# Fixed PSUM banks for the two halves of a convolution block in a four-layer kernel

## Chip, cores and metric

One Trainium2 chip, one core. The time is the device time of one launch in microseconds (us), the median of three runs. The profile is one further execution with the hardware profiler on.

## What is computed

`x` is a float32 tensor (4, 48, 256, 256). Four layers follow each other, each of the form "normalise in 16 groups of 3 channels, apply the layer, add the input". Cut to what matters:

```python
# layer 0: channel attention (48x48) over a 1x1 and a 3x3 depthwise convolution, then a 1x1 projection
x = x + L0(gn(x))
# layer 1: the tensor re-read as tokens of 48 consecutive numbers
t = gelu(gelu(tokens @ W1 + b1))          # 48 -> 16
x1, x2 = t[..., :8], t[..., 8:]
n = layernorm(x2)                         # over 8
g = x1 * (depthwise3x3(n) * pointwise(n))
x = x + (g @ W2 + b2)                     # 8 -> 48, as (h, w, channel)
# layers 2 and 3: four sweeps over rows and columns, each step
# new = input + conv1d(old, w, 5 taps) + b
x = x + L2(gn(x));  x = x + L3(gn(x))
```

Once the attention matrix of layer 0 is known, its output is a 3x3 convolution of the normalised input with weights that the kernel computes per image. That convolution is what "the convolution" means below.

## The kernel before

The work stands in four stretches of the span.

1. 0 to about 1635 us: `products` sums, for each of the four images, the products that the attention needs (L294 to L296).
2. About 1635 to 3205 us: the convolution of layer 0, 64 blocks of 16 rows (16 blocks an image). From about 1980 us the token layer (`gated_layer`, layer 1) runs among it, for images whose convolution is done.
3. 3205 to 3570 us: the rest of the token layer, with the first steps of the sweeps.
4. 3570 us to the end: the sweeps of layers 2 and 3 (`scans`, L1048 and what follows it).

**A convolution block** (`block`, L565) holds eight pairs of rows in four PSUM tiles, numbered c = 0 to 3, each one bank (2 x 256 float32 in each of 96 partitions). `full(c)` (L572) takes a bank and puts three matmuls into it (L582, from `x1n`); `rest(q)` (L586) adds six more matmuls, three each for the tiles q and q + 2 (L591, from `x2n`, 64 partitions each, two at a time on the array). So tiles 0 and 2 are the block's first half, tiles 1 and 3 its second. After `rest`, VectorE adds the input (L605) and takes statistics (L606) of each tile, which frees its bank. The input of the next block is normalised on ScalarE (L542) into `x1n` and `x2n`, of which there is one buffer each.

**The token layer** goes through 32 items in 34 ticks (`tick`). In a full tick one item gets its hidden layer (tiles `ph`, L701), the next one is transposed (`relay` copies the loaded tokens on GpSimd into `pairs`, L748; six tiles `ptok`, L754, of four transposes each, copied to SBUF by VectorE L760 or ScalarE L758), and an older one is gated and written (`psp` and `pch`, L833 to L836; `pm` L788; `pvar` L797, read by ScalarE's L799; eight tiles `pout`, L871, to which VectorE adds the input `xr`, L882, two instructions a tile, after ScalarE's L857 has added the bias to `xr`). A tick calls `conv` four times, and each call is half a block: two blocks a tick.

[...] One (`p_small`) is for small products. Seven are handed out in the convolution and the token layer by a ring of pools:

```python
own = ctx.enter_context(tc.tile_pool(name="a_banks", bufs=5, space=PSUM))
banks = Ring([spare] * 2 + [own] * 5)
```

`Ring.tile` (L125) asks for the pools in turn: two tiles from `spare`, then five from `own`, and so on, whatever the tiles are for. `spare` (2 banks) is later needed by the sweeps of the first pair of images, so when the last convolution half has been handed out (`if not todo`, L646) the ring is cut to `own`.

**The order of instructions** on each engine isn't written by hand. The kernel's text gives a priority order, a planner goes through it with estimated durations, and when an instruction's bank isn't free yet in its plan it takes later instructions first. So the way banks are handed out decides two things: which earlier tile a new one has to wait for, and the order in which TensorE's instructions stand in the program. Each engine then takes its instructions in that order.

## Time and profile before

| | us |
|---|---|
| median of 3 runs | 9344.98 (9341.82 to 9350.19) |
| the profiled execution | 9345.89 |
| its span, first to last instruction | 9344.1 |
| TensorE busy, whole span | 8855.4 (95%) |
| VectorE busy | 4375.0 (47%) |
| ScalarE busy | 3344.1 (36%) |
| GpSimd busy | 1455.0 (16%) |
| mean granted TensorE clock | 0.971 |

The profile's page gives busy time by engine, the span in 40 slices, the chain of work that ended last and the costliest groups of instructions. Beside it the trace answers questions on a stretch: a timeline (start, length, engine, line, operation, and in brackets the idle time before it and what ended it), the waits of one engine added up, and the busy time and granted clock of any window. TensorE's name in these is PE, VectorE's DVE, ScalarE's ACT, GpSimd's POOL; SPq is the queue that issues the DMAs.

### The profile page before, as it was taken

How to read it: one execution, taken by the hardware profiler on the slowest of the kernel's cores; microseconds unless marked ns; L12 is line 12 of the kernel's file. 1: busy time of each engine (PE TensorE's matmuls, PEld its weight loads, DVE VectorE, ACT ScalarE, POOL GpSimd, SP SyncE). 2: the span in 40 equal slices, each digit the busy share in tenths (PEclk: the TensorE clock that was granted, in tenths of full speed). 3: DMA queues.
4: the chain of work that ended last, by engine and by line, in shares of the span. 5: the costliest groups of instructions: out<-in, count | busy, mean ns of one | idle time of the engine just before them, and what ended most of it. 6: DMA issues, size and time to landing. Idle time of an engine off the chain costs nothing.

```text
span 9344.1 us, 160472 instructions
## 1 busy us (share of the span) xinstructions
PE 8855.4 (95%) x62920; PEld 7293.6 (78%) x62920; DVE 4375.0 (47%) x10798; ACT 3344.1 (36%) x7053; POOL 1455.0 (16%) x2866
## 2 busy tenths in 40 slices
PE   6999999999999889999999999999999999999982
PEld 4777777333333348999999999999999999988981
DVE  3331010334555464445666544555677555445541
ACT  0011000123333356645433465555333433445200
POOL 0000000001111120000143200000233333100462
PEclk9999999999999899999999999999999999999996
DMA  7663322568877868666477676654776787697799
GB/s 150 131 131 83 75 65 60 118 138 173 173 167 168 180 151 174 135 143 170 122 173 187 136 159 133 158 140 130 190 190 171 165 193 180 135 213 191 204 217 194
DMA packets 1058039, 1440.82 MB, mean 154 GB/s; under 512 B 64976, under 2 KB 981200, under 8 KB 991232
## 3 DMA queue, kind: packets, MB, share of 16 engines
q1 hardware_dynamic: 1057184, 1430.23, 67.3%
q8 instruction: 493, 8.08, 0.4%
q14 instruction: 266, 2.18, 0.1%
q0 software_dynamic: 96, 0.33, 0.0%
HBM read 837.19 MB, written 534.77 MB: 147 GB/s over the span
## 4 chain that ended last, share of the span: by engine, by line
PE 90%; DMA 4%; DVE 2%; SPq 1%; ACT 1%; issue 1%; POOL 1%; ACTq 0%; DVEq 0%; POOLq 0%
PE ps L1048 57%; PE py L582 7%; PE acc L294 5%; PE acc L295 5%; PE py L591 4%; PE acc L296 4%; PE pt L276 1%; PE ph L701 1%; PE pout L871 1%; PE ptok L754 1%; PE psp L833 1%; DMA oi<-x 1%; DMA tok<-x 1%; DMA sx<-in_x 1%; DMA stage<-x 1%
## 5 line engine op out<-in xcount | busy, mean ns | idle before, releaser
L1048 PE MATMUL ps<-carry,w 96*96 96x128 f32 x48960 | 5588.8, 275 | 91.0 <-DVE carry L1056 60.5
L1048 PEld LDWEIGHTS ps<-carry,w 96*96 96x96 f32 x48960 | 5451.9, 163 | 233.5 <-DVE carry L1056 92.9
L1056 DVE SCALAR_TENSOR_TENSOR carry<-ps,b,col 96x128 f32<-96x128 f32 x4080 | 1777.1, 439 | 1139.7 <-PE ps L1048 964.9
L1261 POOL TENSOR_TENSOR stage<-stage,carry 96x128 f32<-96x128 f32 (+1 forms) x2044 | 1055.3, 520 | 3803.3 <-DVE carry L1056 3621.0
L1231 ACT COPY col<-carry 96x128 f32<-96x128 f32 x2040 | 859.7, 425 | 986.9 <-DVE carry L1056 985.7
L1128 ACT ACTIVATE dn<-carry,b 96x128 f32<-96x128 f32 (+1 forms) x2044 | 791.2, 399 | 1059.2 <-DVE carry L1052 1056.7
L1052 DVE TENSOR_TENSOR carry<-ps,dn 96x128 f32<-96x128 f32 x2280 | 651.6, 287 | 744.9 <-PE ps L1048 571.1
L1052 DVE TENSOR_TENSOR carry<-ps,up 96x128 f32<-96x128 f32 x1792 | 516.3, 288 | 654.0 <-ACT up L1169 491.4
L582 PE MATMUL py<-x1n,wy 128*96 128x512 f32 x1536 | 729.1, 626 | 25.0 <-ACT x1n L542 22.7
L1169 ACT COPY up<-carry 96x128 f32<-96x128 f32 x1792 | 531.0, 298 | 582.3 <-DVE carry L1052 566.5
L294 PE MATMUL acc<-xt 128*96 128x288 f32 x2048 | 666.9, 409 | 0.0
L295 PE MATMUL acc<-xs,xt 128*96 128x288 f32 x2048 | 666.9, 407 | 0.0
L582 PEld LDWEIGHTS py<-x1n,wy 128*96 128x96 f32 x1536 | 255.5, 172 | 457.0 <-issue 443.4
L279 DVE COPY xt<-pt 128x384 f32<-128x384 f32 x256 | 136.5, 554 | 852.2 <-PE pt L276 651.8
L296 PE MATMUL acc<-xt,xs 128*96 128x192 f32 x2048 | 501.7, 327 | 0.0
L261 ACT ACTIVATE xn<-raw,coef 96x2048 f32<-96x2048 f32 x64 | 133.6, 2094 | 985.6 <-PE pt L276 819.1
L296 PEld LDWEIGHTS acc<-xt,xs 128*96 128x96 f32 x2048 | 332.2, 165 | 154.4 <-issue 1.5
L605 DVE TENSOR_TENSOR y<-py,t 96x512 f32<-96x512 f32 x256 | 170.4, 679 | 601.4 <-PE py L591 601.4
L295 PEld LDWEIGHTS acc<-xs,xt 128*96 128x96 f32 x2048 | 332.1, 164 | 151.2 <-issue 2.4
L591 PE MATMUL py<-x2n,wy 64*96 64x512 f32 x1536 | 367.8, 601 | 0.0
L294 PEld LDWEIGHTS acc<-xt 128*96 128x96 f32 x2048 | 330.6, 165 | 5.4 <-issue 1.1
L591 PEld LDWEIGHTS py<-x2n,wy 64*96 64x96 f32 x1536 | 118.3, 158 | 226.4 <-issue 226.2
(177 smaller groups left out, 4194.2 us busy)
## 6 DMA issues: line engine op xcount, KB each, us to landing
stage<-x SPq DMA_DIRECT2D x64, 1536.0 KB
x<-stage SPq DMA_DIRECT2D x64, 1536.0 KB
dn<-x SPq DMA_DIRECT2D x240, 384.0 KB
R<-col SPq DMA_DIRECT2D x60, 1536.0 KB
col<-U SPq DMA_DIRECT2D x60, 1536.0 KB
col<-R SPq DMA_DIRECT2D x60, 1536.0 KB
D<-dn SPq DMA_DIRECT2D x56, 1536.0 KB
up<-D SPq DMA_DIRECT2D x56, 1536.0 KB
```

Source lines behind the costliest of these rows:

```text
L294: nc.tensor.matmul(acc[0], lhsT=xt[:, h + 2, :], rhs=xt[:, here, :], start=first, stop=last)
L295: nc.tensor.matmul(acc[1], lhsT=xt[:, h + 2, :], rhs=xs[:, here, :], start=first, stop=last)
L296: nc.tensor.matmul(acc[2], lhsT=xs[:, h + 2, :], rhs=xt[:, past, :], start=first, stop=last)
L582: nc.tensor.matmul(ps, lhsT=held["w"][0][:, dx], rhs=x1n[:, 2 * c : 2 * c + 2, dx : dx + W], start=dx == 0, stop=False)
L591: nc.tensor.matmul(held["ps"][q + 2 * s], lhsT=held["w"][1][here, dx], rhs=x2n[here, 2 * q : 2 * q + 2, dx : dx + W], start=False, stop=dx ...
L1048: nc.tensor.matmul(ps, lhsT=w_sb[layer][:, way, j, :], rhs=old[:, i, j : j + W // 2], start=j == 0, stop=j == 2)
L1052: nc.vector.tensor_add(new[:, i].rearrange("p (k w) -> p k w", w=KC), ps.rearrange("p (k w) -> p k w", w=KC), inp[:, i])
L1056: nc.vector.scalar_tensor_tensor(new[:, i], ps, b_sb[layer][:, way : way + 1], inp[:, i], ALU.add, ALU.add)
L1128: nc.scalar.activation(inp[:, b], blocks(new[:, b]), AF.Identity, bias=bias[:, 0:1])
L1169: nc.scalar.copy(place[:, b], blocks(new[:, b]))
L1231: nc.scalar.copy(col[:, b], new[:, b])
L1261: nc.gpsimd.tensor_add(to[:, b], to[:, b], new[:, b])
```

## The change

The convolution's first-half tiles (c = 0 and 2) always come from the two `spare` banks. Its second-half tiles (c = 1 and 3) and all tiles of the token layer come from the five `own` banks. The cut of the ring falls away, since nothing but the first halves uses `spare`.

```diff
-    own = ctx.enter_context(tc.tile_pool(name="a_banks", bufs=5, space=PSUM))
-    banks = Ring([spare] * 2 + [own] * 5)
+    banks = ctx.enter_context(tc.tile_pool(name="a_banks", bufs=5, space=PSUM))
...
         def full(c):
...
-            ps = banks.tile([P, 2, W], F32, tag="bank", name="py")
+            ps = (banks if c % 2 else spare).tile([P, 2, W], F32, tag="bank", name="py")
...
     for t in range(-1, n_ticks):
-        if not todo:
-            banks.pools = [own]
         for piece in tick(t, conv, not todo):
             piece()
```

No instruction is added or taken away: the tiles get other banks, and with that another order on TensorE. In the built programs the order of a usual tick is, with F for the six matmuls of two `full` calls (L582), R for the six of a `rest` (L591), and the number of transposes after `ptok`:

```
before  ph psp pch pm  F R  pout2 ptok8 pout2  F R  ptok8 pvar pout4 ptok4  F R  ptok4 F R
after   ph psp pch pm  F R  ptok8 pout4        F R  ptok8 pvar pout4 ptok8  F R  F R
```

(In the third F of the tick before, three of the last four transposes stand between F and R. In the tick after, one matmul of the last F stands already ahead of the third R.) The order from the first tick without convolution to the end of the program is the same in both.

## The prediction, made before the run

> **What bounds the kernel now.** I read the page first, then busy time by stretch, then TensorE's waits in the stretch that the change can touch, then the timeline of one usual tick.

> ```profile
> span 9344.1 us, 160472 instructions
> PE 8855.4 (95%) x62920; PEld 7293.6 (78%) x62920; DVE 4375.0 (47%) x10798; ACT 3344.1 (36%) x7053; POOL 1455.0 (16%) x2866
> PE 90%; DMA 4%; DVE 2%; SPq 1%; ACT 1%; issue 1%; POOL 1%; ACTq 0%; DVEq 0%; POOLq 0%
> ```

> TensorE is the bound, and 57% of the chain that ended last is L1048 in the sweeps, which the change doesn't touch: from the first tick without convolution on, the instructions stand in the same order. What can change lies between about 1960 and 3205 us:

> ```profile
> core 0: us, PE busy (x) PEld busy (x) DVE busy (x) ACT busy (x) POOL busy (x), PEclk, DMA share, GB/s
> 2100.00:3205.50 1105.50, 1041.23 (x3643) 387.79 (x3635) 561.03 (x976) 411.53 (x409) 155.52 (x314) 0.95 0.79 171
> ```

> There TensorE is idle for 64 us of 1105, and its clock is 0.95. TensorE's waits from 1970 to 3210 us (total, number, longest):

> ```profile
> PE ptok L754 <- DVE y L882: 24.1, 20, 4.6
> PE py L582 <- ACT x1n L542: 22.7, 19, 2.9
> PE pout L871 <- DVE y L605: 15.1, 20, 0.9
> PE ptok L754 <- POOL pairs L748: 9.7, 5, 4.5
> ```

> The first three come once a tick. The tick from 2704.14 to 2757.70 us (start, length; idle before in brackets):

> ```profile
> 2718.21 2.82 PE L591 MATMUL py<-x2n,wy 64*96 64x512 f32 x12
> 2721.60 2.87 POOL L748 COPY pairs<-tok 128x1536 f32<-128x1536 f32 x2 [5.10 <-DMA tok<-x]
> 2721.89 1.64 PE L871 MATMUL pout<-g,w_sb 32*96 32x512 f32 x4 [0.86 <-DVE y L605]
> 2723.46 1.09 PE L754 MATMUL ptok<-cst,pairs 128*128 128x128 f32 x8
> 2724.49 1.14 PE L871 MATMUL pout<-g,w_sb 32*96 32x512 f32 x4
> 2725.56 5.39 PE L582 MATMUL py<-x1n,wy 128*96 128x512 f32 x12
> 2725.57 2.00 ACT L857 ACTIVATE xr<-xr,b_sb 96x2048 f32<-96x2048 f32 x1 [0.39 <-DMA xr<-x]
> 2727.60 2.74 DVE L882 TENSOR_TENSOR y<-pout,xr 96x256 f32<-96x256 f32 x8 [2.75 <-ACT xr L857]
> 2735.51 1.41 PE L871 MATMUL pout<-g,w_sb 32*96 32x512 f32 x8
> 2737.24 2.08 ACT L542 ACTIVATE x1n<-t,g 128x2048 f32<-128x2048 f32 x1
> 2737.73 0.63 PE L754 MATMUL ptok<-cst,pairs 128*128 128x128 f32 x4 [0.81 <-DVE y L882]
> 2739.47 7.06 PE L582 MATMUL py<-x1n,wy 128*96 128x512 f32 x12 [1.11 <-ACT x1n L542]
> 2749.21 0.66 PE L754 MATMUL ptok<-cst,pairs 128*128 128x128 f32 x4
> ```

> The reader is to see two sites. **Site 1**, after the first R: `pout` waits for L605 to free the banks of the first half. **Site 2**, after the second: `ptok` waits for a bank that L882 frees, then F for `x1n`. A tick without any slow clock takes 51.9 us (2267.14, 2597.17); most take 53.6 or 55.1, because the clock halves after a site: F at 2739.47 takes 7.06 us where 5.31 is usual. The granted clock in narrow windows, 2200 to 3200 us, shows 17 stretches at 0.50, each costing 1.7 us or a multiple (51.2 in all, some 2.8 a tick).

> [...] stretches begin at 2231.78 and 2341.00 us, 109.22 apart[...]. [...] R: 12 records in 2.82 us when its two halves alternate; a half of R alone, as at 1973.69, has 6 records in 2.81.

> **The change, part by part.** No duration changes; order and waits do. In a usual tick the DMAs on SP's queue and the copies on GpSimd keep their order (the built programs show it), so loads and stores are issued as before. S is a tick's start; S = 2704.14 for the shown one.

> *Site 1.* R ends at S+16.9. Before: 0.86 wait, 1.57 for two `pout` (a second wait, for the second L605, is inside), 1.03 `ptok`, 1.07 `pout`: F at S+21.4. After: `ptok8` comes first, and has no bank wait, but `pairs` is not there. GpSimd copies it in two halves of 1.46 from the moment the token DMA lands, 17.3 after S in most ticks (2721.60 here), so `ptok` can start at S+18.8. The DMA is issued off the tick's start and isn't moved. Then 1.03[...]: F at S+21.6. The wait for L605 (15.1 in the stretch) is gone, and a wait of about 1.9 for `pairs`, hidden so far by `pout2`, is there instead: +0.1 to +0.2 a tick.

> *A new wait in the second F.* Its second matmul group takes the bank of the first `pout`, which two L882 free, and these wait for ScalarE's L857. F's first group takes 2.65, so the second is due at S+24.2. L857 runs S+21.4 to S+23.4 (bound by the `xr` DMA), two L882 take 0.7: S+24.15. Zero, with no reserve. Behind it would queue R and all of TensorE. Bounds: 0 to 1.3, since L857 starts between S+20.9 and S+22.2 in the ticks of before. I take 0.

> *Site 2.* The four `pout` now use banks that L605 (two), L758 and L760 free, done 0.7, 2.1, 1.7 and 2.7 after R's end; they are due 1.9, 2.2, 2.5 and 2.9 after it: no wait. `ptok` waits for L882 as before (0.8), but eight transposes run in the gap instead of four; the last four need `pvar`'s bank, free when L799 ends (S+33.3), before they are due. F starts when L542 ends, as before. So 0.49 us of transposes go into a wait of 1.11 and are gone from S+45: −0.49. Of the other engines ScalarE's copy (0.58) moves ahead of `x2n`'s L542, which then ends at about S+41.0, and R, behind seven matmul groups, is due at S+41.6: hidden, with 0.6 left. VectorE's L760 (0.68) moves ahead of L903; L605 is due 2 us after that ends.

> A usual tick: +0.15 − 0.49 = −0.35. There are 21 ticks with `pout` and convolution; two of them (2319, 2757) keep their order at site 2. 19 × −0.35 = −6.6 us.

> *The start.* Three stretches before the ticks are full. Before, F and R stand ahead of `ptok` and cover the token DMA; after, `ptok8` stands right behind `pm` or R. Prelude (1963): R ends at 1971.4, `pairs` gives at 1980.97: a wait of 9.6 where 4.47 was; against it two halved R at full cost (1.4 each) go; with its clock +3.5. Tick at 2007.64: `ptok` due at S+12.5, given at about S+18: +5.5, less the waits of 0.76 and 2.93 that go; a clock window more: +2. Tick at 2053.86: due S+12.5, given S+18.2, 5.7 of idle where none was, less two halved R (2.8), plus a slow stretch (3.4): +6. Sum +11.5; bounds +4 (DMA lands earlier, as half of it is issued earlier in one tick) and +16.

> *The clock.* Before, 2.8 us a tick. After, site 1 has one idle time of 1.9 and then light work, against pieces of 0.86 and 0.6; site 2 has 1.5 idle instead of 1.9. Low windows become likelier at site 1, rarer at site 2. A tick of 51.5 is 15.1 windows (51.9: 15.2), so it comes back at nearly the same phase. I take 0; bounds: every tick one window (1.7: −21 us over 19), every tick two (3.4: +12).

> Sum: −6.6 + 11.5 + 0 + 0 = +5 on the profiled execution's 9345.9 (its span 9344.1 and 1.8 around it). That execution is 0.9 above the median; on the median, 9345 + 4 = **9349 us**.

> **Rivals.**
> - *The clock settles at one window a tick or none* (site 2 clean, site 1 in step with the windows): −21 − 6.6 + 11.5, about 9328; with half the ticks clean, 9310. For it: ticks without any exist (51.9). Against: the idle time at site 1 gets longer in one piece.
> - *The second F waits at the bank of the first `pout`* (the slower side). Price: what L857 starts later than S+21.4, per tick, 21 ticks. It decides from about 0.7 us on: 21 × 1.0 + 4 = +25, 9370; with the extra slow windows that such a gap brings (+12), 9382. For it: in three ticks L857 does start near S+22.2, and a DMA share of 0.79 leaves little room. Against: those are ticks where TensorE is late too.
> - *Nothing moves* because TensorE's order follows the DMAs anyway: 9345. For it: site 1 ends within 0.2 us where it ended. Against: the start loses its cover for sure.

> **How the numbers follow.** A measurement of this kernel can tell about 0.2% (18.7 us) from no change. Forecast near 9349: 0.56. Clock rival: 0.16. Second-F rival: 0.20. Nothing moves: 0.08. Range 9328 to 9374: bounds of start and clock, into both rivals. The forecast and "nothing" stay within 0.2% but for some 0.06 above; about 0.01 of the clock rival stays inside. Faster 0.15, same 0.59, slower 0.26.

> **What would show it.** Right: `pout` no longer waits for L605; `ptok` waits some 1.9 us for `pairs` in every tick; L882's wait at site 2 remains; ticks without slow clock near 51.5; the stretch before 2100 about 11 us longer. Wrong: F waiting for L882, `pvar` or `ptok` for L799; R waiting for `x2n`; a clock of this stretch above 0.97 or below 0.94; any difference after the last convolution half.

## The result, and the profile after

| | before | after |
|---|---|---|
| median, us | 9343.70 (9341.82 to 9350.19, 4 runs) | 9303.15 (9300.01 to 9315.16, 4 runs) |
| the profiled execution, its span | 9345.89, 9344.1 | 9302.44, 9300.7 |
| mean granted TensorE clock | 0.971 | 0.975 |

The ratio is 0.9958, with a 95% interval of 0.994 to 0.9975: the change makes the kernel 0.42% faster. The forecast was 9349, its range 9328 to 9374. It was wrong on the side of the gain.

Line numbers of the changed kernel are three lower than before in the token layer (`pout` L868, `ptok` L751, `y` L879) and one lower in the convolution (F L581, R L590). First the page, the same lines as before, then the stretch of the twenty ticks with convolution and `pout`, from the start of the third tick to the end of the last R (before: 2097.1 to 3205.5).

```profile
span 9300.7 us, 160515 instructions
PE 8807.2 (95%) x62920; PEld 7274.7 (78%) x62920; DVE 4378.6 (47%) x10798; ACT 3355.6 (36%) x7053; POOL 1454.7 (16%) x2866
PE 87%; DMA 6%; DVE 2%; SPq 2%; ACT 1%; issue 1%; POOL 1%; ACTq 0%; DVEq 0%; POOLq 0%
```

```profile
core 0: us, PE busy (x) PEld busy (x) DVE busy (x) ACT busy (x) POOL busy (x), PEclk, DMA share, GB/s
2103.50:3159.10 1055.60, 998.08 (x3670) 371.67 (x3671) 564.33 (x980) 420.79 (x409) 155.80 (x316) 0.99 0.82 179
```

The working instructions of every engine are as many as before; the 43 more in the span are of the sequencers, which wait and issue. TensorE is busy 48 us less than before with the same 62920 matmuls, and its clock in the twenty ticks is 0.99, not 0.95. That is nearly the whole result: over the whole span the half clock costs 270 us in before and 232 in after, 39 of the 43 us by which the spans differ. I measured the loss to the half clock by cutting the stretch into windows of 0.4 us and adding up length times (1 − granted clock):

| us | before | after | difference |
|---|---|---|---|
| third tick starts at | 2097.1 | 2103.5 | +6.4 |
| twenty ticks | 1108.4 | 1055.6 | −52.8 |
| of these, half clock | 59.7 | 8.5 | −51.2 |
| of these, the rest | 1048.7 | 1047.1 | −1.6 |
| last R to last `pout` | 354.8 | 358.4 | +3.6 |
| from there to the end of the span | 5783.8 | 5783.2 | −0.6 |

The waits changed in kind more than in sum: in the twenty ticks TensorE idles 64.3 us in before and 57.5 in after. Its waits from 1970 to 3165 us:

```profile
PE ptok L751 <- POOL pairs L745: 31.3, 16, 10.2
PE py L581 <- ACT x1n L541: 27.9, 33, 1.1
PE pout L868 <- DVE xt L757: 7.4, 10, 1.1
PE pstrip L718 <- DVE strip L720: 4.6, 2, 2.3
PE ptok L751 <- DVE y L879: 4.6, 18, 1.0
```

`pout` no longer waits for the convolution's bank, as foretold. F waits for `x1n` 33 times, not 19: in thirteen ticks the first F waits too. And `pout` waits ten times for VectorE's copy L757, which empties a bank of `ptok`. A tick of after, to be held against the one of before:

```profile
2694.09 5.36 PE L581 MATMUL py<-x1n,wy 128*96 128x512 f32 x12 [1.13 <-ACT x1n L541]
2699.38 2.82 PE L590 MATMUL py<-x2n,wy 64*96 64x512 f32 x12
2702.21 1.09 PE L751 MATMUL ptok<-cst,pairs 128*128 128x128 f32 x8
2703.23 1.15 PE L868 MATMUL pout<-g,w_sb 32*96 32x512 f32 x6
2705.35 1.14 PE L868 MATMUL pout<-g,w_sb 32*96 32x512 f32 x2 [0.97 <-DVE xt L757]
2706.42 5.39 PE L581 MATMUL py<-x1n,wy 128*96 128x512 f32 x12
...
2716.37 2.01 PE L868 MATMUL pout<-g,w_sb 32*96 32x512 f32 x8
2718.59 1.06 PE L751 MATMUL ptok<-cst,pairs 128*128 128x128 f32 x8 [0.21 <-DVE y L879]
2720.34 6.22 PE L581 MATMUL py<-x1n,wy 128*96 128x512 f32 x14 [0.68 <-ACT x1n L541]
```

The tick starts at S = 2683.96. The idle time that the profile shows now lies in small pieces in three places: 1.13 ahead of the first F, 0.97 within `pout`, 0.21 and 0.68 at site 2. Why the first F waits is seen on ScalarE. Of before, and then of after:

```profile
2710.34 2.05 ACT L542 ACTIVATE x1n<-t,g 128x2048 f32<-128x2048 f32 x1
2712.30 0.67 ACT L839 ACTIVATE sp<-psp,col 128x512 f32<-128x512 f32 x1
```

```profile
2691.28 0.69 ACT L836 ACTIVATE sp<-psp,col 128x512 f32<-128x512 f32 x1 [0.91 <-PE psp L831]
2691.86 2.08 ACT L541 ACTIVATE x1n<-t,g 128x2048 f32<-128x2048 f32 x1
```

With other banks the planner has put the copy of `psp` ahead of the normalisation, and that copy stands idle until `psp` is done.

```profile
2228.38:2231.80 3.42, 2.55 (x12) 0.93 (x9) 2.48 (x4) 0.00 (x0) 2.53 (x2) 1.00 1.11 211
2231.80:2235.21 3.41, 3.41 (x11) 1.52 (x10) 0.69 (x1) 2.22 (x2) 0.34 (x1) 0.50 1.13 203
2235.21:2238.62 3.41, 3.41 (x5) 1.13 (x5) 2.74 (x8) 2.19 (x2) 0.00 (x0) 0.50 1.13 207
```

```profile
2733.55:2736.97 3.42, 3.37 (x20) 1.62 (x18) 3.21 (x6) 2.18 (x3) 0.45 (x3) 1.00 0.20 56
2736.97:2740.38 3.41, 1.54 (x6) 0.83 (x7) 3.41 (x4) 2.36 (x2) 0.00 (x0) 1.00 0.88 205
2740.38:2743.79 3.41, 3.41 (x6) 1.11 (x5) 3.38 (x8) 1.71 (x2) 0.00 (x0) 0.50 0.01 4
```

```profile
2716.16:2719.57 3.41, 3.20 (x17) 1.58 (x16) 3.41 (x7) 3.38 (x4) 0.31 (x1) 1.00 0.59 115
2719.57:2722.99 3.42, 2.74 (x8) 1.08 (x8) 3.42 (x4) 0.67 (x2) 0.00 (x0) 1.00 0.40 115
2722.99:2726.40 3.41, 3.41 (x9) 1.11 (x7) 3.41 (x8) 3.39 (x4) 0.31 (x1) 1.00 0.02 3
```

The first number after the length is TensorE's busy time, the number after the engines its granted clock. At site 2 of before, one window has 1.54 of 3.41 us busy, and the next is granted 0.50; that costs 1.7 us. In the tick of after none of the three windows is below 2.74. At site 1 of before, a window with 2.55 us busy is followed by two at half clock; 1.64 of the 2.55 us are `pout`, which the experiments come back to. By place, the loss of before in the twenty ticks is 44.3 us at site 1 (12 stretches, each of two slow windows or more) and 15.4 at site 2 (7 stretches); in after it is 8.5, all at site 1.

### The profile page after: what moved, and what is told of

Its sections match the earlier page's. It is cut to its first block, busy times and chain, and to the rows that moved or that the text cites. A ratio compares the mean times of both kernels' runs of the same rounds, so it can differ in the third digit from the quotient of the medians.

```text
span 9300.7 us, 160515 instructions
## 1 busy us (share of the span) xinstructions
PE 8807.2 (95%) x62920; PEld 7274.7 (78%) x62920; DVE 4378.6 (47%) x10798; ACT 3355.6 (36%) x7053; POOL 1454.7 (16%) x2866
## 4 chain that ended last, share of the span: by engine, by line
PE 87%; DMA 6%; DVE 2%; SPq 2%; ACT 1%; issue 1%; POOL 1%; ACTq 0%; DVEq 0%; POOLq 0%
PE ps L1045 57%; PE py L581 6%; PE acc L294 5%; PE acc L295 5%; PE acc L296 4%; PE py L590 3%; DMA tok<-x 1%; PE pt L276 1%; DMA oi<-x 1%; PE ptok L751 1%; PE pout L868 1%; DMA col<-R 1%; PE ph L698 1%; ACT x1n L541 1%; DMA sx<-in_x 1%
## 5 line engine op out<-in xcount | busy, mean ns | idle before, releaser
L581 PE MATMUL py<-x1n,wy 128*96 128x512 f32 x1536 | 700.8, 605 | 29.6 <-ACT x1n L541 27.9
L581 PEld LDWEIGHTS py<-x1n,wy 128*96 128x96 f32 x1536 | 243.7, 165 | 451.0 <-issue 434.4
L590 PE MATMUL py<-x2n,wy 64*96 64x512 f32 x1536 | 363.0, 601 | 0.0
L590 PEld LDWEIGHTS py<-x2n,wy 64*96 64x96 f32 x1536 | 116.9, 159 | 233.7 <-issue 231.1
```

The lines of the kernel that those rows point to most:

```text
L581: nc.tensor.matmul(ps, lhsT=held["w"][0][:, dx], rhs=x1n[:, 2 * c : 2 * c + 2, dx : dx + W], start=dx == 0, stop=False)
L590: nc.tensor.matmul(held["ps"][q + 2 * s], lhsT=held["w"][1][here, dx], rhs=x2n[here, 2 * q : 2 * q + 2, dx : dx + W], start=False, stop=dx ...
```

## The experiments

All but the unused matmuls of some of them leave the computation as it is. The site at which a stretch of half clock begins is given by its start in the tick: up to S+30 site 1, later site 2. In the table, "loss" is that to the half clock in the twenty ticks, by site, and "rest" is their length without it, both from the one profiled execution, which need not be near the median (e2's is the slowest of four, 9318.94; e7's is 13 us above its median, e3's 11 below); "ratio" is to the kernel before in the same batch, with its interval. "Piece" is the usual longest idle time at site 1.

| run | site 1: piece, `pout` | site 2: transposes ahead of F | loss 1 / 2 | rest | median, us | ratio |
|---|---|---|---|---|---|---|
| before | 0.87, two and two | 4 | 44.3 / 15.4 | 1048.7 | 9343.70 | 1 |
| after | up to 1.4, four | 8 | 8.5 / 0 | 1047.1 | 9303.15 | 0.9958 [0.994, 0.9975] |
| e1_fill | filled, two and two | 4, filled | 3.4 / 1.7 | 1059.9 | 9309.90 | 0.9962 [0.9947, 0.9977] |
| e2_pout_after_ptok | 1.6 to 2.2, four | 4 | 18.7 / 18.7 | 1030.6 | 9298.00 | 0.9951 [0.9935, 0.9967] |
| e3_pout_split | 1.9, two and two | 6 | 61.4 / 0 | 1060.9 | 9377.01 | 1.0032 [1.0021, 1.0043] |
| e4_ptok_spare | 1.7, four | 4 | 15.4 / 13.6 | 1046.1 | 9325.21 | 0.9983 [0.9975, 0.9991] |
| e5_sp_dve | 1.2 to 2.0, four | 8 | 13.7 / 1.7 | 1031.1 | 9301.43 | 0.9955 [0.994, 0.997] |
| e6_start_cover | as after | 8 | 11.9 / 0 | 1047.8 | 9305.32 | 0.9958 [0.9941, 0.9974] |
| e7_two_fills | 1.6, filled, four | filled, then F | 0 / 0 | 1108.5 | 9356.42 | 1.0011 [1.0004, 1.0018] |
| e8_fill_site1 | 1.0, filled, four | 4 | 5.1 / 8.6 | 1036.1 | 9301.53 | 0.9948 [0.9934, 0.9961] |
| e9_fill_both_sites | 1.0, filled, four | 4, filled | 5.1 / 0 | 1036.4 | 9285.97 | 0.9933 [0.992, 0.9945] |
| e10_site2_back | 1.5 to 2.1, four | 4 | 17.1 / 13.6 | 1042.7 | 9327.00 | 0.9977 [0.9968, 0.9985] |
| e11_after_again | as after | 8 | 15.4 / 1.7 | 1047.0 | 9307.94 | 0.9963 [0.995, 0.9975] |
| e12_fill_again | as e9 | 4, filled | 3.4 / 0 | 1035.1 | 9286.23 | 0.994 [0.9927, 0.9952] |

### Is it the idle time at the two sites that halves the clock?

e1_fill keeps the banks and the order of before and puts four unused matmuls into the waits, two behind R at site 1, ahead of the first `pout`, and two behind the last `pout` of site 2.

```diff
+            if ip == 0 and q == 0 and not alone:
...
+                fill(512)
+                fill(256)
...
+        if ip == 1 and not alone:
+            fill(512)
+            fill(512)
```

> The kernel before, with four extra matmuls a tick whose result nobody uses, in places where TensorE waits: 1.3 us of them between the first R and pout, 1.7 us between the last pout and the transposes of site 2. Banks and order are those of before. Clock theory (the gain of the change is fewer windows at half clock): the half-clock loss from 2100 to the last convolution half falls from about 60 us to under 15, and the time to about 9295 (9285 to 9310). Bank theory (the gain is the bank waits themselves, the clock only follows the kernel's other limits): no wait's end moves, so 9344 or up to 10 more.

Measured: 9309.90; the loss falls from 59.7 to 5.1 us, and the rest grows by 11. More work, no change of banks, and most of the gain: the clock is the cause, and these two places set it.

### Which part of the change is it, banks or order?

e2_pout_after_ptok keeps the ring of seven banks and changes the order of site 1 alone: each first `pout` is issued behind the eighth transpose.

```diff
+            with tc.issue_after(hook["ptok"].ins) if ip == 0 and not alone else ExitStack():
                 nc.tensor.matmul(
...
```

> The kernel before with its ring of seven banks; only the order at site 1 is that of after: the four pout stand behind the eight transposes. Clock theory: site 1 ends no earlier, but its low windows go, some 40 of 60 us of half-clock loss; site 2 keeps its own (1.7 us in every second or third tick); 9315 (9305 to 9330). Bank theory: the banks are those of before, so 9344 within 8.

Measured: 9298.00, the gain of the whole change without its banks, and more than either theory had said. Its four runs lie far apart, 9285.73 to 9318.94; the clock over the whole span was 0.977 in the first and 0.973 in the second of these, which at 9300 us is about 37 us, enough for all of the difference. The profiled execution is the slowest of the four. One of its ticks, with S = 2261.45:

```profile
2275.52 2.82 PE L591 MATMUL py<-x2n,wy 64*96 64x512 f32 x12
2280.42 1.23 PE L757 MATMUL ptok<-cst,pairs 128*128 128x128 f32 x8 [2.08 <-POOL pairs L751]
2281.58 2.03 PE L875 MATMUL pout<-g,w_sb 32*96 32x512 f32 x8
...
2296.25 0.63 PE L757 MATMUL ptok<-cst,pairs 128*128 128x128 f32 x4 [0.81 <-DVE y L886]
2297.99 2.54 PE L582 MATMUL py<-x1n,wy 128*96 128x512 f32 x3 [1.12 <-ACT x1n L542]
```

Here is what the prediction expected of after: `ptok` waits 2.1 us for `pairs` in one piece. Half clock begins at site 1 ten times. Yet this costs less than the two pairs of `pout` of before: 18.7 us of loss at site 1, not 44.3, though TensorE idles longer in these ticks, 76.7 us in all against 64.3. And the rest of the ticks is 18 us shorter: with the half clock taken off, the `pout` of site 1 take 23 us in the twenty ticks where they took 58, as four run side by side and no bank is waited for among them.

e3_pout_split goes the other way: the banks of after, and `pout` in two pairs among the transposes again (site 2 also changed, to six transposes and two).

```diff
...
+            pieces.append(lambda: transposed(c + 1, 0))
+        if was and not alone:
+            pieces.append(lambda: pouts(old, 0, range(2)))
+        if new:
+            pieces.append(lambda: transposed(c + 1, 1))
```

> The kernel after with its fixed banks; at site 1 the four pout stand in two pairs with four transposes before each. Clock theory, if it is the pairs that make windows low: 10 to 35 us of half-clock loss come back, 9315 to 9340. Bank theory: banks as after, 9303 within 8.

Measured: 9377.01, slower than before and than the 9315 to 9340 expected; the loss is back at 61.4 us, all at site 1, and the rest is 14 us longer than in after. With `pout` in pairs, the fixed banks gain nothing.

### How much lies in each site?

e4_ptok_spare gives the sixth `ptok` tile of the twenty ticks a bank of `spare`.

```diff
-        pt = banks.tile([128, 4, 128], F32, tag="bank", name="ptok")
+        pt = (spare if i == 5 and c in range(3, 23) else banks).tile([128, 4, 128], F32, tag="bank", name="ptok")
```

> The kernel after; the last of the six ptok tiles comes from the two banks of the first halves, so that four transposes, not eight, stand in the gap of site 2 and four come back behind R. Both theories: 0.5 us a tick more (10 us). Clock theory beside it: site 2's windows get low again, 1.7 us in every third tick, 9303 + 10 + 12 = 9325. Bank theory: 9313.

Measured: 9325.21, the number expected, but not as it was made up: against after the loss is 20.5 us larger, at both sites, and the rest 1 us shorter, not 10 longer. The planner made more of it than the one bank: at site 2 four transposes stand ahead of F again, and the first F no longer waits for `x1n`, so that `pairs` is waited for in one piece. So this run can't tell the two sites apart.

e10_site2_back takes the order of site 2 alone back to that of before.

```diff
-        for q in range(4):
+        behind = tc.issue_after(hook["R"].ins) if i == 5 and c in range(3, 23) else ExitStack()
+        with behind:
+          for q in range(4):
             nc.tensor.transpose(pt[:, q, :], m[:, q, 128 * i : 128 * i + 128], k["ident", 128])
```

> The changed kernel with one part of its order undone: at site 2 four transposes instead of eight stand between pout and F, the other four behind R, as in the kernel before. Theory (a window under half busy makes the next one slow): the idle time there would be about 0.2 + 1.2 us around 0.63 us of transposes, about 0.58 busy, so no slow windows come with it; the loss in the ticks stays under 15 us, and only the 0.46 us of transposes that no longer lie in the wait are added, 18 times: 8 us, 9305 to 9318. Rival (the eight transposes at site 2 are what keeps the clock up): 10 to 18 windows of 1.7 us more, 9325 to 9335.

Measured: 9327.00, a loss of 30.7: the rival was right, though with 8 slow windows at site 2 and not 10 to 18. Site 2 has 13.6 us of loss, where after has none and its repeat 1.7. Site 1 has 17.1, hardly more than the 15.4 of that repeat. A window of site 2 and the next:

```profile
2244.54:2247.96 3.42, 2.08 (x13) 0.77 (x8) 3.42 (x6) 3.18 (x3) 0.00 (x0) 1.00 0.81 172
2247.96:2251.37 3.41, 3.41 (x5) 1.14 (x6) 3.41 (x7) 0.89 (x1) 0.00 (x0) 0.50 0.20 66
```

The window is 0.61 busy, as I had reckoned, and is followed by half clock all the same. Of its 2.08 us busy, 1.37 are `pout`, whose matmuls use 32 of 128 rows each (32*96 in the records, where F has 128*96). So the busy time of the records is not the measure; rows in use may enter it.

I therefore took all windows of the grid that ran at full clock in the twenty ticks, of these traces, of after and of the two repeats below: 4213 windows in 14 traces, 124 of them followed by half clock (a few windows change places in the table with the way the ends of records are cut). With `pout` counted at half its time (the weight that splits them best, 0.5 of those between 0 and 1 that I tried):

| busy share, `pout` at half | followed by half clock |
|---|---|
| under 0.40 | 59 of 63 |
| 0.40 to 0.48 | 48 of 80 |
| 0.48 to 0.52 | 13 of 57 |
| 0.52 to 0.60 | 3 of 122 |
| over 0.60 | 1 of 3891 |

Without that weight, 37 windows of over 0.60 are followed by half clock; each of the 37 holds 0.84 us or more of `pout`.

One weight for all `pout` is too coarse. Their records also show how many run side by side at each moment, and each uses 32 rows. Counted as a quarter of the time where one runs alone, a half for two, three quarters for three and the whole for four (the share of the 128 rows in use), the split is far sharper. Of the 4199 windows that lie wholly within the ticks:

| busy share, `pout` by rows in use | followed by half clock |
|---|---|
| under 0.46 | 111 of 116 |
| 0.46 to 0.50 | 11 of 47 |
| over 0.50 | 2 of 4036 |

Run by run too, the windows under 0.46 are about as many as the stretches of half clock: 20 to 19 in before, 4 to 4 in after, 14 to 16 in e10. By this count the window of e10 above is 0.43 busy, since 0.65 of its 1.37 us of `pout` are one alone, the fourth, which came late. The window of 2.55 us at site 1 of before is 0.43 as well: a single `pout` for 1.10 us, two for 0.51. Of the weights tried for one to four side by side, those of the rows rank the windows best, and counting the transposes at half, or R at three quarters, makes the split worse. It is a fit to these traces, not an experiment: no run changed the rows of a matmul and nothing else.

### Does the length of one piece of idle time decide?

e5_sp_dve takes the copy of `psp` from ScalarE to VectorE, so that the first F needn't wait for `x1n`.

```diff
-        nc.scalar.activation(sp, flat(psp), AF.Identity, bias=col[:, 4:5])
+        nc.vector.tensor_scalar_add(sp, flat(psp), col[:, 4:5])
```

> The changed kernel, but VectorE instead of ScalarE adds the bias to psp, so that the copy into x1n isn't queued behind it and the first F of a tick needn't wait (1.14 us in some 15 ticks of the changed kernel). Theory (what sets the half clock is how much idle time falls together): F starts 1.1 us earlier, but the token DMA lands where it did, so the wait for pairs at site 1 grows from some 0.8 to some 1.9 us in one piece; nothing is gained in waits and half-clock stretches come back at site 1 in a third to two thirds of the ticks: loss in the ticks from 8.5 to 20 to 35 us, time 9310 to 9325. Rival (each wait costs its own length and no more): the 1.14 us are gone in 15 ticks, 17 us, the loss stays near 8.5, time 9287.

Measured: 9301.43, no different from after, and neither theory whole. TensorE's waits in the twenty ticks (2107.2 to 3153.8 us):

```profile
PE ptok L751 <- POOL pairs L745: 25.9, 17, 2.0
PE py L581 <- ACT x1n L541: 13.1, 20, 0.8
PE pout L868 <- DVE xt L757: 1.3, 2, 0.7
```

The wait did move to `pairs`, in one piece of up to 2.0 us, and the loss at site 1 did rise, from 8.5 to 13.7, less than I had said, and no more than the repeat of the changed kernel showed of itself (15.4): that the pieces of idle time are smaller in after is not shown to matter. But `pout` hardly waits for L757 any more (1.3 us), and the rest is 16 us shorter. Of this, 4 us were lost ahead of the third tick, 7 to the clock, and 7 behind the last R. With e10 it shows site 2 by itself: the wait for `pairs` is in one piece in both, eight transposes stand at site 2 here and four there, and the loss at site 2 is 1.7 against 13.6.

### Is the start worth anything?

e6_start_cover puts two halves of a convolution in front of the first transposes, in the stretches before the third tick.

> The changed kernel, but in the three stretches ahead of the third tick two convolution halves stand together in front of the first transposes, so that they cover the token DMA. Theory: the start returns to that of the kernel before (third tick at 2097 instead of 2103.5) and the ticks keep their loss of 5 to 15 us: 9297. Rival (the ticks came out at a lucky phase against the clock's windows, and a start moved by 6 us puts them at another): loss in the ticks 25 us or more, 9315 to 9325.

Measured: 9305.32. The third tick starts at 2092.3, 11 us earlier than in after, more than expected; the loss of the ticks is 11.9. The time isn't better: 4 us go in the ticks and 8 behind the last R. The stretch from there to the last `pout` took 353 to 363 us in the fourteen traces and what follows 5783 to 5797, whatever the ticks did; differences below some 10 us can't be followed to the end.

### A version that beats both

e7_two_fills: the seven banks of before, `pout` behind the transposes, three unused matmuls ahead of `ptok` at site 1 and four behind `pout` at site 2.

> The kernel before with its ring of seven banks; at site 1 the order is R, three unused matmuls of 512 columns, eight transposes, four pout, and at site 2 four unused matmuls stand between the last pout and F, with the eight last transposes behind that F. Seven of 0.43 us, 3.0 us a tick, in waits that add up to some 4.6 us (2.1 for pairs; 0.8, 0.63 of transposes and 1.1 at site 2). Theory: they are hidden, the ticks keep the length that the run with pout behind the transposes had without its slow clock (1031 us for twenty) and lose 5 to 10 us to half clock; the third tick starts at 2097: ticks 1038 to 1045, time 9278 to 9287, faster than the changed kernel. Rival (the half clock isn't set by these two sites, or the matmuls push what follows): 9298 or slower.

Measured: 9356.42, a miss, and not for the clock: not one window at half clock in the twenty ticks (PEclk 1.00), but the rest of the ticks is 78 us longer than in e2. An unused matmul of 512 columns takes 0.91 us (three take 2.74), two records of 0.46; I had reckoned 0.43. At 6.4 us a tick they no longer fitted into the waits.

e8_fill_site1 and e9_fill_both_sites are the same with the right size: 0.9 us ahead of `ptok` at site 1 (one matmul of 512 columns in e8, two of 256 in e9), and in e9 alone one of 256 behind the last `pout` of site 2. Of e9:

```diff
+        if ip == 1 and not alone:
+            fills(1)
...
+        if was and not alone:
+            pieces.append(lambda: [hook.update(last=hook["R"]), fills(2)])
```

> The kernel before with pout behind the eight transposes at site 1, as in the run that did this alone, and one unused matmul of 512 columns (0.91 us, as the seven of the run before took) inside the wait of 2.1 us for pairs at site 1; site 2 is left as it was before. Theory (a clock window in which TensorE is less than about half busy is followed by a window at half clock): the window at site 1 goes from 0.35 to 0.5 busy up to 0.6 or more, its 9 slow windows of that run go, the 11 of site 2 (0.44 busy) stay: loss in the ticks 15 to 22 us, the ticks without it 1031 to 1035, time 9280 to 9292. Rival (the sites share one cause, or the matmul lengthens the path): loss above 30 us or ticks above 1045, time 9298 or more.

> The same, with 0.9 us of unused matmuls at site 1 (two of 256 columns) and 0.45 us (one of 256) between pout and the four transposes of site 2, where 0.8 and 1.1 us were idle around 0.63 us of transposes. Theory: busy share at site 2 from 0.44 to 0.55, at site 1 above 0.6, so hardly a slow window in the ticks: loss below 6 us, ticks without it 1031 to 1038, third tick at 2097, time 9268 to 9282, the fastest of all. Rival: the matmuls aren't hidden (then 20 times up to 1.35, 27 us, on the ticks: 9290 to 9300), or the clock isn't a matter of these two windows (loss above 20 us).

Measured: 9301.53 and 9285.97. With site 1 filled, its loss is 5.1, where e2 had 18.7; with both filled it is 5.1 and 0. But at site 2, which e8 leaves alone, the loss is 8.6 where e2 had 18.7 and where it was expected to stay, so one execution of each can't put the whole fall at site 1 down to the fill; and e8's median is no better than the 9298.00 of e2. It is the fill at site 2 that shows in the time: 16 us from e8 to e9, which also splits the fill of site 1 in two. e8 is 10 us and e9 4 us above what was expected, in a batch in which the kernel before took 9350.45, against 9341 to 9348 in the others. TensorE in a tick of e9, S = 2671.60:

```profile
2688.42 1.13 PE L711 MATMUL fill<-w_sb,dw_sb 128*128 128x256 f32 x4
2690.65 1.09 PE L772 MATMUL ptok<-cst,pairs 128*128 128x128 f32 x8 [1.10 <-POOL pairs L764]
2691.67 1.15 PE L893 MATMUL pout<-g,w_sb 32*96 32x512 f32 x8
2692.76 5.39 PE L583 MATMUL py<-x1n,wy 128*96 128x512 f32 x12
...
2704.05 0.70 PE L711 MATMUL fill<-w_sb,dw_sb 128*128 128x256 f32 x2
2704.93 0.63 PE L772 MATMUL ptok<-cst,pairs 128*128 128x128 f32 x4 [0.18 <-DVE y L908]
2706.67 5.36 PE L583 MATMUL py<-x1n,wy 128*96 128x512 f32 x12 [1.11 <-ACT x1n L542]
```

The fill of site 1 lies in the wait for `pairs`, that of site 2 in the wait for L908 (L882 of before). To compare it with the change, both ran again side by side:

> The changed kernel itself, unchanged, on the same chip as the next one, to compare the two: 9303, a loss in the ticks of 5 to 20 us.

> The fastest kernel so far (seven banks, pout behind the transposes at site 1, 1.35 us of unused matmuls a tick), again, beside the changed kernel: 9280 to 9290, and 12 to 20 us below the changed kernel on the same chip; if the gain was that chip's, no difference.

The changed kernel took 9307.94 (0.9963 of before, 0.995 to 0.9975), the filled one 9286.23 (0.994, 0.9927 to 0.9952): 22 us less. No run of the one overlaps with a run of the other. The loss was 17.1 and 3.4 us. So the loss of the changed kernel isn't fixed either: 8.5 in one execution, 17.1 in another, with the same idle time in the ticks (57.5 and 57.8). What the change takes from the half clock is thus 43 to 51 us by these two, against the one trace of before.

## Why the prediction was wrong, step by step

**The clock, "I take 0": the step that failed.** Measured −51.2 us, and a clock of 0.99 in this stretch, where the prediction had named anything above 0.97 as a sign of being wrong. The whole gain is in this term. Two things in it were false.
- "Low windows become likelier at site 1": I compared idle times, 1.9 in one piece against 0.86 and 0.6. What had made the windows of before low was more than these: the two pairs of `pout`, 1.57 (with a wait inside) and 1.07 us. One `pout` alone takes 1.14 (2705.35 in after), two take 1.14, three 1.15 (2703.23) and four 1.15 (e9): standing together costs nothing, so two pairs are twice the time at half the rows or fewer, and by the rows in use the windows that hold them go low. The order of e2, which has the idle piece of 2.1 us that the prediction feared, still takes the loss of site 1 from 44.3 to 18.7; putting the pairs back (e3) brings it to 61.4.
- The bound of −21 allowed at best one window a tick. The rival "settles at one window a tick or none" came nearest, with its clean site 2, but it left site 1 at one window a tick or half the ticks, was reckoned to 9328 or 9310, and was given 0.16. The profile of before held 2.8 us a tick, some 56 us, that could go; the bound should have reached that far.

**Site 1, F at S+21.6.** Measured S+22.5 (2706.42), where before had S+21.4. Three terms were off. The first F waits 1.13 for `x1n`: not foreseen; I had followed TensorE's, SP's and GpSimd's order, but not ScalarE's. The wait for `pairs`, 1.9 in the sum, is 0 to 1.8, mostly below 1, as F's delay hides part of it. Four `pout` were put at 1.75, an estimate that no trace shows (site 2 of before has 1.41): they take 1.15 where they stand together, but in ten ticks the fourth waits up to 1.05 for L757 and then takes another 1.07 by itself, 3.2 us in the tick shown. So the tiles of four run side by side: 1.15 us for all (e9), 1.14 for one alone.

**The second F, "I take 0".** Right but for one tick (0.3 us). The rival that ended slower wasn't there.

**Site 2, −0.49.** Right: F comes 5.85 us after the first transpose (2714.49 to 2720.34) with sixteen of them in between, against 5.84 with twelve before (2733.63 to 2739.47), so four of 0.49 us have gone into the wait. It is divided otherwise than I said, 0.21 for L879 and 0.68 for `x1n`, with the same end. "No wait" for the four `pout` was not so: they take 2.01 (2716.37) where they took 1.41, 0.6 more for their banks, which the wait for `x1n` hides. That it would also end the slow windows of this site, worth 15.4 us, wasn't in the sum.

**The usual tick, −0.35.** Without slow clock it went from 51.9 to 52.5, since site 1 took 1.1 more. Against this, the two ticks with `pstrip` fell from 54.1 and 54.0 to 52.0 and 51.7, as a wait of 4.62 for L882 went and one of 2.31 for `strip` came; I had left these two out of the sum. There are also only twenty ticks with `pout` and convolution, not 21: the tick of 2097.11 is the first and that of 3150.36 the last. Over the twenty −1.6; the sum had −6.6 for nineteen.

**The start, +11.5.** Right in sign and within its bounds: +6.4. But all of it is half clock, 6.8 us more from 1900 us to the third tick (13.7 against 6.8); the longer waits (one of 10.24 for `pairs` where 4.47 was) are made up elsewhere, in the first stretch by the halved R that went (two of 2.81 us before, none after). By stretch it is +1.9, 0 and +4.4, where the prediction had +3.5, +2 and +6; the middle one, by the figures given for it, should have come to +3.5.

**The stretch after the last convolution half.** I had called any difference there a sign against me. There is one of 3.6 us, of about the size in which this stretch varies from trace to trace.

## What to carry over

On a TensorE that is 95% busy, look not only at how long it waits but at what its clock does after each wait: here 64 us of idle time came with another 60 us of half clock, and a change that took only 7 us from the idle time took 51 from the half clock (43 in the repeat). Put work with few rows together, so that its tiles run side by side, and fill a wait that leaves a 3.4 us window less than about half busy, few rows counted for less (under 0.46 to 0.50 in the second table of e10), if the fill fits into the wait; and where a bound is set for such a loss, let it reach to the whole of what the profile holds.

## What was unexpected of the hardware

- A window with idle pieces of 0.81 and 1.11 us, and 0.63 us of transposes between, was followed by one at half clock (site 2 of before: 1.54 of 3.41 us busy, then a granted clock of 0.50). The half clock went with how much of one window of the grid was busy: of the windows under 0.46, `pout` counted by its rows, 111 of 116 were followed by half clock, of those over 0.50 2 of 4036.
- 32-row matmuls, alone or in pairs, didn't keep the clock up, though the profile shows TensorE busy: windows of 0.75 busy by the records (2.55 of 3.41 us) were followed by half clock in before. Counted by the rows in use they fall in with the others (0.43 for the one shown).
- A slow window costs 1.7 us (half of 3.4133), and in before each stretch at site 1 had two or three; the half-clocked window after the one shown held light work again, two `pout` for 2.02 us from 2232.88. A tick of e2 without slow clock is 51.2 us, 15.0 windows, and with two slow windows by this reckoning 54.6, 16.0 (54.8 to 55.0 in its trace): a tick that has them meets the grid in nearly the same place next time. That may be how runs of this one program come to lie 33 us apart; with one trace of it, this is not shown.
